# Start of an attention-and-experts kernel: order of the first loads, weight norms from row statistics, first block's roots and the shared splits on VectorE, second block's roots next

## The chip, the cores and the metric

The kernel runs on one core of one Trainium2 chip. The metric is device time in microseconds (us) of one execution; lower is better. The number given for a kernel is the median of its runs.

## The reference

The input x has 4 x 2048 rows of 512. It is layer-normalised to xn, and the output is x + attention(xn) + experts(xn).

- Attention by random features: for a row v, feature r is exp(ab[r] * (v . gs[r]) - 0.5 * |v|^2 * ab[r]^2) times a constant of r, with 512 features. The same function is applied to the 512 rows of `input_weights`, and the output is the product of the rows' features with the features of these weights. So two things are needed of each set of rows: its product with `proj_matrix`, and its squared norms.
- Experts: scores over 64 experts in 8 groups, the best 4 groups, the best 8 experts in them, at most 256 rows per expert; for every expert silu(gate) * up and a down product; plus one shared expert for all rows.

```
dot_products = einsum('...d,rd->...r', xw, ab[:, None] * gs)
correction = (0.5 * sum(xw * xw, axis=-1))[..., None] * (ab * ab)
return 1.0 / sqrt(NUM_RFS) * AB * exp(dot_products - correction)
```

## The kernel before, in words

Tensors are float32. Every large product is made of three passes on TensorE: each operand is split into a rounded high part (`upper`, L96, a cast on ScalarE) and a rest (`rest`, L99, a subtraction, on VectorE unless it is told otherwise), and `products` (L102) multiplies high by high, high by low and low by high.

The rows are worked in 16 blocks of 512 (4 tiles of 128). For each block:

- `normalize` (L252): row statistics on VectorE (`bn_stats`, L257, `bn_aggr`, L261), then the inverse root of the variance in `inverse_root` (L221): two integer operations on VectorE for a first guess (L225, L226) and three Newton steps of four tiny GpSimd operations each (L228 to L231). Two more GpSimd operations make `shift` (L268, L269), three the squared norms (L271 to L273). Then ScalarE writes the four normalised tiles `xw` (L276).
- `look_up` (L309): a generator. Its first step turns the block (`turn`, L291: 16 transposes on TensorE through PSUM, L299, four casts on ScalarE and four subtractions on VectorE give `xT_h` and `xT_l`). Later steps make the router's logits (`ps_l`, L327), copy them (`lt`, L337), turn them back (`ps_lt`, L344) and choose groups and experts with many VectorE operations (L352 to L401), count rows per expert (`ps_b`, `ps_u`, L406, L417) and store the normalised rows and the counts.
- `dense` (L473), for even blocks before the experts: shared gate and up products (`ps_gu`, 48 matmuls), the features (`ps_f`, 48 matmuls, each group of 12 followed by `exponent`, L450, on VectorE and an Exp on ScalarE), and the shared down and attention products (`ps_o`). Odd blocks get this between and after the experts.

`routing` (L790) is called after each step of `dense`; it moves the generators on, starts a block's `look_up` at a step counted by GAP = 5, and calls `normalize` for the block after it. After the 16 blocks, 64 experts follow, then a rest.

The order on each engine comes from the tile framework, which schedules what the program lists and what its dependencies and `behind` (L116: an order without a wait) demand. Every engine works through its list in order. [...]

What is before the first block (L158 to L175 and L572 to L630):

- Loads on the SP queue, in this order: `xis`, `proj_matrix` (`pj`), `input_weights` (`wi`), block 0, router weights, the three shared weights (`sgu` twice, `sd`). Then 1.1 MB of zero rows are written. Block 1 is loaded after the weights' products have been listed (L616).
- `pT` and `wT` are turned from `pj` and `wi`. The weights' squared norms are four ScalarE squares with an accumulator (L583); they are padded, transposed on VectorE, written to `norms` in memory by four small DMAs (`as_row`, L238) and read back over all partitions (`across`, L246: tile `q`).
- The weights' projection: four groups of 12 matmuls `ps_f` in the pool `ps_mm`, each followed by `exponent` into `fw` (L452), which needs `q`.
- The rests of the shared weights are made on GpSimd:

```
    shared_gu = split_gates(sgu, nc.gpsimd, (squared, root))
    ...
    shared_w = shared_gu, split_down(sd, nc.gpsimd)
```

PSUM has three pools: `ps_tr` (2 tiles), `ps_mm` (4) and `ps_sm` (2).

Of the kernel before, what the change touches and what calls it, by code (L numbers as in the profile page):

```python
# [9 lines left out]
FP = mybir.dt.float32  # L10
# [42 lines left out]
def rfs_attention_moe_kernel(  # L53
# [106 lines left out]
    nc.sync.dma_start(ab, xis.rearrange("(c p) -> p c", p=P))  # L160
    pj = load_rows(proj, "pj")
    wi = load_rows(iw, "wi")
# [4 lines left out]
    def load_shared():  # L167
        sgu = [kib4([P, KC, I], "sgu", FP) for _ in range(2)]
        for t, w in zip(sgu, (sgw, suw)):
            nc.sync.dma_start(t, w.rearrange("(c p) i -> p c i", p=P))  # L170
        sd = kib4([P, IC, H], "sd", FP)
        nc.sync.dma_start(sd, sdw.rearrange("(c p) h -> p c h", p=P))
        return sgu, sd

    sgu, sd = load_shared()  # L175
# [45 lines left out]
    def inverse_root(y, v):  # L221

        a = rt.tile([P, NS], FP, tag="a", name="a", bufs=2)
        yi = y.bitcast(I32)
        nc.vector.tensor_scalar(yi, v.bitcast(I32), 1, None, ALU.logical_shift_right)  # L225
        nc.vector.tensor_scalar(yi, yi, -1.0, float(0x5F3759DF), ALU.mult, ALU.add)  # L226
        for _ in range(3):
            nc.gpsimd.tensor_tensor(a, y, v, ALU.mult)  # L228
            nc.gpsimd.tensor_tensor(a, a, y, ALU.mult)
            nc.gpsimd.tensor_scalar(a, a, -0.5, 1.5, ALU.mult, ALU.add)  # L230
            last["root"] = nc.gpsimd.tensor_tensor(y, a, y, ALU.mult)  # L231
# [20 lines left out]
    def normalize(b):  # L252
        xb = xbs[b]
        mv = rt.tile([P, NS, 2], FP, tag="mv", name="mv", bufs=2)
        for s in range(NS):
            st = rt.tile([P, 6], FP, tag="st", name="st", bufs=4)
            stats = nc.vector.bn_stats(st, xb[s])  # L257
            if b == 0:
                behind(stats, last["rest"])
            last["stats"] = stats  # L260
            nc.vector.bn_aggr(mv[:, s, :], st)  # L261
        ve = rt.tile([P, NS], FP, tag="ve", name="ve", bufs=2)
        nc.vector.tensor_scalar(ve, mv[:, :, 1], EPS, None, ALU.add)
        rstd = rt.tile([P, NS], FP, tag="rstd", name="rstd", bufs=2)
        inverse_root(rstd, ve)

        shift = rt.tile([P, NS], FP, tag="shift", name="shift", bufs=2)
        nc.gpsimd.tensor_tensor(shift, mv[:, :, 0], rstd, ALU.mult)  # L268
        nc.gpsimd.tensor_scalar(shift, shift, -1.0, None, ALU.mult)  # L269
# [3 lines left out]
        nc.gpsimd.tensor_scalar(padded[b % 2][:, :NS], q1, -0.5 * H, None, ALU.mult)  # L273
        xw = [rows.tile([P, NH, XW], FP, tag="xw", name="xw") for _ in range(NS // NH)]
# [34 lines left out]
    def look_up(b):  # L309
# [5 lines left out]
            ((ps_tr, "tr"), (ps_sm, "sm")),  # L315
# [134 lines left out]
    def exponent(dst, v, nsq, rc, ps):  # L450
        products(ps, parts(pT, KC, ts(rc, P)), v, True, True)
        return nc.vector.scalar_tensor_tensor(  # L452
            dst, nsq, ab[:, rc : rc + 1], ps, ALU.mult, ALU.add
        )
# [7 lines left out]
    def feature(fT, v, nsq, rc, ps):  # L462
        f = act.tile([P, TB], FP, tag="t", name="f")
        exponent(f, v, nsq, rc, ps)
        nc.scalar.activation(f, f, AF.Exp, scale=ab[:, rc : rc + 1])
        upper(fT[0][rc], f)
        last["dve"] = rest(fT[1][rc], f, fT[0][rc])
# [103 lines left out]

    pT = turn(lambda s: pj[s], "pT", ((ps_mm, "mm"),))  # L572
    wT = turn(lambda s: wi[s], "wT", ((ps_tr, "tr"), (ps_sm, "sm")))
# [4 lines left out]
    normed[0] = normalize(0)  # L578
    first, root = last["stats"], last["root"]
    wq = const.tile([P, NS], FP, name="wq")  # L580
    for s in range(NS):
        sq = act.tile([P, H], FP, tag="t", name="sq")
        squared = nc.scalar.activation(sq, wi[s], AF.Square, accum_out=wq[:, s : s + 1])  # L583
        behind(squared, last["upper"])
    nc.vector.tensor_scalar(padded[2][:, :NS], wq, -0.5, None, ALU.mult)
    as_row(NB, padded[2])
    wn = across(NB)

    def split_gates(gu, on=nc.vector, after=None):
        hi = [kib4([P, KC, I], "gu_h") for _ in range(2)]  # L590
        lo = [kib4([P, KC, I], "gu_l") for _ in range(2)]
        for n in range(2):
            a = upper(hi[n], gu[n])
            b = rest(lo[n], gu[n], hi[n], on)
            if after is not None:
                behind(a, after[0])
                behind(b, after[1])
        return hi, lo

    def split_down(d, on=nc.vector):  # L600
        dh = kib4([P, IC, H], "d_h")
        dl = kib4([P, IC, H], "d_l")
        upper(dh, d)
        rest(dl, d, dh, on)
        return dh, dl

    shared_gu = split_gates(sgu, nc.gpsimd, (squared, root))
    fw = Chunks(RC, "fw", FP)
    for rc in range(RC):
        ps = ps_mm.tile([P, H], FP, tag="mm", name="ps_f")  # L610
        exponent(fw[rc], parts(wT, KC), wn, rc, ps)
# [4 lines left out]
    xbs[1] = load_tokens(1)  # L616
    late = look_up(0)
    next(late)
    normed[1] = normalize(1)
    next(late)  # L620
    next(late)
    shared_w = shared_gu, split_down(sd, nc.gpsimd)
    fW = Chunks(RC, "fW_h"), Chunks(RC, "fW_l")

    def features_w(rc):
        f = fw[rc]
        nc.scalar.activation(f, f, AF.Exp, scale=ab[:, rc : rc + 1])
# [162 lines left out]
    def routing(t):  # L790
# [5 lines left out]
        if k == 0 and b < NB:  # L796
            fronts[b] = look_up(b)
            next(fronts[b])
        if k == GAP - 3 and b + 1 < NB:
            normed[b + 1] = normalize(b + 1)  # L800
# [35 lines left out]
    def ends():  # L836
# [15 lines left out]
        raw, w = load_shared(), []  # L852
# [85 lines left out]
```

## Time and profile before

| | |
|---|---|
| median of 3 runs | 1355.71 us (1353.23 to 1357.19) |
| profiled execution | 1351.38 us, span 1349.6 us |
| TensorE busy | 1322.5 us (98% of the span) |
| VectorE busy | 919.5 us (68%) |
| ScalarE busy | 647.1 us (48%) |
| GpSimd busy | 580.0 us (43%) |
| mean granted clock of TensorE | 0.993 |

The profile is of one execution. In it PE is TensorE's matmul, PEld its weight load, DVE VectorE, ACT ScalarE, POOL GpSimd, SP the queue that issues most DMAs. L12 is line 12 of the kernel. A line of the timeline has the start, the length, the engine, the line, the operation, out<-in with shapes, and in brackets the idle time before it with what ended it. A line of the stages has the stretch, its length, and busy time (count) of PE, the granted clock, the share of time in which the DMA engines were busy, and what they moved; where it lists all engines, they are PE, PEld, DVE, ACT and POOL in that order. A line of the waits has who waited for whom, us in total, how often, and the longest.

### The profile page before, as it was taken

The page shows a single profiled execution, that of the slowest core. Times are in us where ns is not written, and L with a number is a line of the kernel's source. Part 1 is how long each engine was busy: PE and PEld are TensorE (multiplying, and loading weights), DVE is VectorE, ACT ScalarE, POOL GpSimd, SP SyncE. Part 2 cuts the span into 40 slices and gives each one's busy share as a digit, 9 for nine tenths or more (in the row PEclk, how much of TensorE's full clock was granted, in tenths as well). Part 3 has the DMA queues.
Part 4 walks back from the last instruction along what each step waited for, and adds up shares of the span by engine and source line. Part 5 has one row for each costly group of instructions (what it writes and reads, how often), then busy time and mean ns, then how long its engine had stood idle before and what let it go on. Part 6 is the DMA issues. An engine that isn't in the chain of part 4 may idle for free.

```text
span 1349.6 us, 21219 instructions
## 1 busy us (share of the span) xinstructions
PE 1322.5 (98%) x7648; PEld 1153.4 (85%) x7648; DVE 919.5 (68%) x1898; ACT 647.1 (48%) x1025; POOL 580.0 (43%) x683
## 2 busy tenths in 40 slices
PE   7899999999999899999999999999999999999998
PEld 5788888888888799999999999999999999978886
DVE  5887768768765577767677777767776776544455
ACT  5554433443432365556555655655665566531111
POOL 3322022022004566777667676767677655220000
PEclk9899999999999999999999999999999999999999
DMA  7464544564476899999999999999999989756995
GB/s 248 173 231 166 211 184 157 210 222 161 169 268 200 261 243 286 277 270 272 289 268 257 299 287 263 247 283 286 266 263 289 280 235 273 200 143 231 306 316 203
DMA packets 186265, 327.06 MB, mean 242 GB/s; under 512 B 15536, under 2 KB 87216, under 8 KB 186160
## 3 DMA queue, kind: packets, MB, share of 16 engines
q1 hardware_dynamic: 153392, 245.93, 53.0%
q0 software_dynamic: 32768, 79.78, 26.6%
q8 instruction: 60, 0.98, 0.3%
q14 instruction: 45, 0.37, 0.1%
HBM read 220.66 MB, written 104.99 MB: 241 GB/s over the span
## 4 chain that ended last, share of the span: by engine, by line
PE 91%; DMA 3%; DVE 2%; POOL 2%; ACT 1%; issue 1%; SPq 0%; DVEq 0%; POOLq 0%; ACTq 0%
PE ps_gu L107 40%; PE ps_e L107 13%; PE ps_o L107 13%; PE ps_f L107 6%; PE ps_y L107 5%; PE ps_fu L107 5%; PE ps_t L717 4%; PE ps_l L327 2%; PE ps_x L299 2%; DMA at<-upto,line 1%; DMA rw_sb<-in_L_ffn_router_w_dram 1%; POOL at L649 1%; DMA xT_l<-turned 1%; PE ps_lt L344 0%; DVE r L460 0%
## 5 line engine op out<-in xcount | busy, mean ns | idle before, releaser
L107 PE MATMUL ps_gu<-gT,gu_h 128*128 128x256 f32 x2048 | 295.1, 284 | 0.0
L767 POOL DMA_INDIRECT out_dram<-ye,who x128 | 217.4, 1698 | 142.0 <-DMA out_dram<-ye,who 41.1
L107 PEld LDWEIGHTS ps_gu<-gT,gu_h 128*128 128x128 f32 x2048 | 269.3, 192 | 7.0 <-ACT gu_h L97 2.5
L702 POOL DMA_INDIRECT xg<-xnw,who x128 | 143.4, 1121 | 96.1 <-issue 72.1
L649 POOL DMA_INDIRECT at<-upto,line x128 | 148.0, 1156 | 82.5 <-DVE xb L506 43.8
L107 PE MATMUL ps_gu<-gT,gu_l 128*128 128x256 f32 x1024 | 167.1, 285 | 0.0
L100 DVE TENSOR_TENSOR gu_l<-gu,gu_h 128x1024 fp32r<-128x1024 f32 x128 | 155.4, 1216 | 3.8 <-ACT gu_h L97 3.8
L107 PE MATMUL ps_e<-d_h,ehT 128*128 128x512 f32 x512 | 148.8, 392 | 0.0
L107 PEld LDWEIGHTS ps_gu<-gT,gu_l 128*128 128x128 f32 x1024 | 140.9, 192 | 2.8 <-DVE gu_l L100 2.7
L97 ACT CAST gu_h<-gu 128x1024 fp32r<-128x1024 f32 x128 | 131.5, 1056 | 0.0
L97 ACT CAST ehT<-sg 128x512 fp32r<-128x512 f32 x64 | 39.8, 622 | 179.2 <-DVE sg L460 179.2
L228 POOL TENSOR_TENSOR a<-rstd,ve 128x4 f32<-128x4 f32 x48 | 10.9, 227 | 265.4 <-DVE rstd L226 262.8
L107 PEld LDWEIGHTS ps_e<-d_h,ehT 128*128 128x128 f32 x512 | 94.9, 188 | 19.0
L766 ACT ACTIVATE ye<-ps_e,we 128x512 f32<-128x512 f32 x128 | 87.9, 693 | 33.9 <-PE ps_e L107 33.9
L460 DVE SCALAR_TENSOR_TENSOR sg<-sg,ps_gu 128x512 f32<-128x512 f32 x64 | 44.0, 688 | 81.5 <-PE ps_gu L107 81.2
L100 DVE TENSOR_TENSOR d_l<-d,d_h 128x1024 fp32r<-128x1024 f32 x64 | 78.2, 1222 | 11.3 <-ACT d_h L97 11.2
L458 ACT ACTIVATE sg<-ps_gu 128x512 f32<-128x512 f32 x64 | 38.2, 597 | 96.2 <-PE ps_gu L107 95.6
L100 DVE TENSOR_TENSOR gT<-ps_t,gT 128x512 fp32r<-128x512 f32 x128 | 83.3, 682 | 0.4 <-ACT gT L97 0.4
L107 PE MATMUL ps_e<-d_l,ehT 128*128 128x512 f32 x256 | 79.1, 390 | 1.0 <-DVE d_l L100 1.0
L107 PE MATMUL ps_o<-fW_h,fT 128*128 128x512 f32 x288 | 79.7, 391 | 0.3 <-ACT fT L97 0.2
L107 PE MATMUL ps_o<-d_h,hT 128*128 128x512 f32 x256 | 79.8, 399 | 0.0
L717 PE MATMUL ps_t<-ident,xg 128*128 128x128 f32 x512 | 76.1, 275 | 3.5 <-DVE gT L100 3.5
(172 smaller groups left out, 2534.2 us busy)
## 6 DMA issues: line engine op xcount, KB each, us to landing
gu<-in_L_ffn_gate_w_dram SPq DMA_DIRECT2D x64, 512.0 KB
gu<-in_L_ffn_up_w_dram SPq DMA_DIRECT2D x64, 512.0 KB
d<-in_L_ffn_down_w_dram SPq DMA_DIRECT2D x64, 512.0 KB
xnw<-xw SPq DMA_DIRECT2D x32, 577.0 KB
xb<-in_L_attn_x_dram SPq DMA_DIRECT2D x32, 512.0 KB
out_dram<-xb SPq DMA_DIRECT2D x32, 512.0 KB
xT_h<-turned SPq DMA_DIRECT2D x30, 512.0 KB
xT_l<-turned SPq DMA_DIRECT2D x30, 512.0 KB
```

Of the source, the lines that this page charges most:

```text
L97: return nc.scalar.copy(dst, src)
L100: return on.tensor_tensor(dst, src, hi.bitcast(FP), ALU.subtract)
L107: last["pe"] = nc.tensor.matmul(ps, w[c][a], v[c][b], start=(start and part == 0 and c == 0), stop=(stop and part == 2 and c == n - 1),)
L299: last["turn"] = nc.tensor.transpose(ps[:, ts(s, P)], src(s)[:, ts(kc, P)], ident)
L327: logits = nc.tensor.matmul(pl, rwp[:, kc].rearrange("p t e -> p (t e)"), v[kc], start=(n == 0 and kc == 0), stop=(n == 1 and kc == KC - 1),)
L458: nc.scalar.activation(dst, g, AF.Tanh, scale=0.5)
L460: nc.vector.scalar_tensor_tensor(dst, dst, 0.5, u, ALU.mult, ALU.mult)
L649: nc.gpsimd.indirect_dma_start(out=at[:, e % TE, h, :], out_offset=None, in_=upto, in_offset=bass.IndirectOffsetOnAxis(ap=line[:, e, h : h ...
L702: nc.gpsimd.indirect_dma_start(out=xgs[e][:, h, :], out_offset=None, in_=xnw, in_offset=bass.IndirectOffsetOnAxis(ap=who[:, e, h : h + 1], ...
L717: turned_s = nc.tensor.transpose(ps[:, c, ts(h, P)], xg[:, h, ts(c2 * 2 + c, P)], ident)
L766: nc.scalar.activation(ye[:, h, :], po, AF.Copy, scale=wes[e][:, h : h + 1])
L767: now = nc.gpsimd.indirect_dma_start(out=out, out_offset=bass.IndirectOffsetOnAxis(ap=who[:, e, h : h + 1], axis=0), in_=ye[:, h, :], in_o ...
```

## The change

- Loads: `wi` before `pj`; block 1 after the router weights and before the shared weights.
- The weights' squared norms come from `bn_stats` and `bn_aggr` on VectorE (mean squared plus variance, times 512, on GpSimd) in place of the four ScalarE squares. `wT` is turned before `pT`.
- `normalize` is cut into `statistics`, `roots` and the rest. Block 0's Newton steps and its `shift` are on VectorE; all other blocks' stay on GpSimd. Block 1's statistics and roots are listed right after block 0's.
- All three rests of the shared weights are on VectorE: gate's behind block 1's first guess, up's and down's behind block 0's `xT_l`. The casts of up and down go behind block 0's `xT_h`.
- The weights' projection uses `ps_sm` and `ps_tr`, and its `exponent` goes behind block 0's `xT_l`; block 0 is turned through `ps_mm`. 
- Block 1's `look_up` starts one step later.

On the engines: in the changed program GpSimd has 14 operations fewer and VectorE 24 more; on ScalarE the four squares are gone. From VectorE's 180th operation or so on (block 2), the lists of all engines are those of before.

```
+    wi = load_rows(iw, "wi")
     pj = load_rows(proj, "pj")
-    wi = load_rows(iw, "wi")
...
+    xbs[1] = load_tokens(1)
+    sgu = load_shared_gates()
+    sd = load_shared_down()
...
-    def inverse_root(y, v):
+    def inverse_root(y, v, on):
...
-            nc.gpsimd.tensor_tensor(a, y, v, ALU.mult)
-            nc.gpsimd.tensor_tensor(a, a, y, ALU.mult)
-            nc.gpsimd.tensor_scalar(a, a, -0.5, 1.5, ALU.mult, ALU.add)
-            last["root"] = nc.gpsimd.tensor_tensor(y, a, y, ALU.mult)
+            on.tensor_tensor(a, y, v, ALU.mult)
+            on.tensor_tensor(a, a, y, ALU.mult)
+            on.tensor_scalar(a, a, -0.5, 1.5, ALU.mult, ALU.add)
+            on.tensor_tensor(y, a, y, ALU.mult)
...
-            ((ps_tr, "tr"), (ps_sm, "sm")),
+            ((ps_tr, "tr"), (ps_sm, "sm")) if b else ((ps_mm, "mm"),),
...
+    wmv = statistics(wi)
+    wT = turn(lambda s: wi[s], "wT", ((ps_tr, "tr"), (ps_sm, "sm")))
+    wq = const.tile([P, NS], FP, name="wq")
+    nc.gpsimd.tensor_tensor(wq, wmv[:, :, 0], wmv[:, :, 0], ALU.mult)
+    nc.gpsimd.tensor_tensor(wq, wq, wmv[:, :, 1], ALU.add)
+    nc.gpsimd.tensor_scalar(padded[2][:, :NS], wq, -0.5 * H, None, ALU.mult)
...
-    normed[0] = normalize(0)
-    first, root = last["stats"], last["root"]
-    wq = const.tile([P, NS], FP, name="wq")
-    for s in range(NS):
-        sq = act.tile([P, H], FP, tag="t", name="sq")
-        squared = nc.scalar.activation(sq, wi[s], AF.Square, accum_out=wq[:, s : s + 1])
-        behind(squared, last["upper"])
...
+    normed[0] = normalize(0, *roots(0, statistics(xbs[0], NS * [last["rest"]]), nc.vector))
+    first = last["shift"]
+    roots1 = roots(1, statistics(xbs[1], NS * [first]))
+    seed1 = last["seed"]
+
+    def split(t, name, after=(None, None)):
+
+        hi, lo = kib4(list(t.shape), name + "_h"), kib4(list(t.shape), name + "_l")
+        for a, b in zip((upper(hi, t), rest(lo, t, hi)), after):
+            if b is not None:
+                behind(a, b)
+        return hi, lo
...
-    shared_gu = split_gates(sgu, nc.gpsimd, (squared, root))
+    sgate = split(sgu[0], "gu", (None, seed1))
+    ps_w = []
+    for rc in range(RC):
+        pool, tag = ((ps_sm, "sm"), (ps_tr, "tr"))[rc // 2]
+        ps_w.append(pool.tile([P, H], FP, tag=tag, name="ps_f"))
+        projected(parts(wT, KC), rc, ps_w[rc])
+    late = look_up(0)
+    next(late)
+    upper0 = last["upper"]
+    sup = split(sgu[1], "gu", (upper0, last["rest"]))
+    shared_w = list(zip(sgate, sup)), split(sd, "d", (upper0, last["rest"]))
     fw = Chunks(RC, "fw", FP)
     for rc in range(RC):
-        ps = ps_mm.tile([P, H], FP, tag="mm", name="ps_f")
-        exponent(fw[rc], parts(wT, KC), wn, rc, ps)
+        behind(exponent(fw[rc], wn, rc, ps_w[rc]), last["rest"])
+    normed[1] = normalize(1, *roots1)
...
-    xbs[1] = load_tokens(1)
-    late = look_up(0)
-    next(late)
-    normed[1] = normalize(1)
...
-    shared_w = shared_gu, split_down(sd, nc.gpsimd)
...
-        if k == 0 and b < NB:
+        if k == (b == 1) and b < NB:
...
-            normed[b + 1] = normalize(b + 1)
+            normed[b + 1] = normalize(b + 1, *roots(b + 1, statistics(xbs[b + 1])))
```

## Prediction

> **What bounds it now.** I read the first part of the page, then TensorE's waits, then the first 100 us by stages, then the timeline around TensorE's gaps.
>
> ```profile
> span 1349.6 us, 21219 instructions
> PE 1322.5 (98%) x7648; PEld 1153.4 (85%) x7648; DVE 919.5 (68%) x1898; ACT 647.1 (48%) x1025; POOL 580.0 (43%) x683
> ```
>
> TensorE is busy for all but 27 us. Its waits:
>
> ```profile
> PE ps_x L299 <- ACT xw L276: 6.9, 5, 4.5
> PE ps_x L299 <- DMA pj<-_L_attn_proj_matrix_dram: 5.9, 2, 5.3
> ```
>
> 5.9 us are the first load; 6.9 us are waits for the normalised tiles of blocks 0 and 1. By stages (TensorE alone, then all engines):
>
> ```profile
> 23.20:26.60 3.40, 1.01 (x4) 0.93 0.84 305
> 26.60:29.70 3.10, 3.08 (x14) 0.52 0.79 297
> ...
> 39.70:44.20 4.50, 0.03 (x2) 0.89 0.34 124
> 44.20:49.20 5.00, 5.00 (x20) 0.50 0.00 0
> ```
>
> ```profile
> 60.00:70.00 10.00, 10.00 (x51) 8.01 (x50) 9.43 (x23) 7.95 (x16) 4.58 (x17) 1.00 0.77 276
> 70.00:80.00 10.00, 9.97 (x50) 7.89 (x49) 10.00 (x43) 3.87 (x9) 0.00 (x0) 1.00 0.38 130
> 80.00:90.00 10.00, 10.00 (x47) 8.22 (x46) 9.57 (x41) 4.64 (x9) 6.44 (x29) 1.00 0.57 207
> ```
>
> Each wait is followed by a stretch at half the clock (0.52, 0.50). And from 60 to 90 us VectorE is as full as TensorE: there it has little room for a lead. What ends the waits:
>
> ```profile
> 17.47 0.20 POOL L228 TENSOR_TENSOR a<-rstd,ve 128x4 f32<-128x4 f32 x1 [2.72 <-DVE rstd L226]
> 17.75 0.20 POOL L229 TENSOR_TENSOR a<-a,rstd 128x4 f32<-128x4 f32 x1
> ...
> 20.70 2.39 POOL L100 TENSOR_TENSOR gu_l<-sgu,gu_h 128x1024 fp32r<-128x1024 f32 x1
> ...
> 23.64 2.93 ACT L276 ACTIVATE xw<-xb,shift,rstd 128x512 f32<-128x512 f32 x4 [5.35 <-POOL shift L269]
> ...
> 25.41 2.73 DVE L452 SCALAR_TENSOR_TENSOR fw<-q,ab,ps_f 128x512 f32<-128x512 f32 x4 [8.02 <-DMA q<-norms]
> ...
> 36.62 2.36 DVE L226 TENSOR_SCALAR rstd<-rstd 128x4 int32<-128x4 int32 x1
> ...
> 43.32 2.93 ACT L276 ACTIVATE xw<-xb,shift,rstd 128x512 f32<-128x512 f32 x4 [6.14 <-POOL shift L269]
> ```
>
> Block 0's roots run on GpSimd at one operation per 0.28 us (17.47 to 17.75) and have a 2.4 us shared split among them. Block 1's come late: statistics on VectorE at 32.03, the first guess (L226) held for 2.36 us beside GpSimd's split of `sd`, then roots to 43.3.
>
> What the two gaps cost: without waits, 16 transposes take 1.7 us (the row at 93.20). Gap A: products of weights end at 23.2, block 0's first product starts at 29.54, so 29.54 - 23.2 - 1.75 = 4.6 us. Gap B: from 39.56 to 50.15 TensorE does 16 transposes and 7 matmuls, 1.75 + 7 x 0.227 = 3.35 us, so 10.6 - 3.35 = 7.2 us. Together 11.8 us, the most that the change can give.
>
> **The change, part by part.**
>
> Loads. `wi` takes `pj`'s place (5.3 and 6.5 us), `pj` that of `wi` (10.2). TensorE's first 32 transposes keep their times. The four `bn_stats` with aggregates of `wi` (4 x 0.66 + 4 x 0.16 = 3.3 us) fill 5.3 to 8.3, where VectorE is idle (its first split is at 7.91); it is back in step at `pT_l`, 11.3 to 13.8, as `wT_l` before. Block 0's statistics stay at 13.8 to 16.7. The ScalarE squares (2.5 us) are hidden now and are worth nothing. Later loads: before, 5.97 MB have moved by 19.5 us at about 350 GB/s; block 1's 1.05 MB goes ahead of the shared weights and puts these 3 us later: first gate at about 17, `sd` at 19.5, zero rows until 22.5. Their casts are needed from 25 us on, so this is covered.
>
> Block 0's roots on VectorE. 12 + 2 operations. No row has this form on VectorE; the nearest, L225 to L226 (17.02 to 17.22), are dependent and tiny too: 0.20 us. The bounds are 0.17 (the duration alone) and 0.28 (GpSimd's). 14 x 0.20 = 2.8 us: 17.25 to 20.05. `xw` then takes 20.1 to 23.0 and is there when the weights' products end at 23.2. Gap A's wait goes, and with it the cold stretch; transposes end at 24.95.
>
> What is late next: ScalarE's casts `xT_h` (0.56 each, the last at 25.95) and `gu_h` of up (27.0). VectorE has block 1's statistics first (20.05 to 22.8, guess to 23.3), gate's rest (1.22, from the row of the same form at L100 for experts, in place of GpSimd's 2.39) to 24.55, `xT_l` 4 x 0.62 to 27.0. The first 24 gate and up matmuls (5.45 us) end at 30.9: 0.5 us lost.
>
> Block 1's roots stay on GpSimd, from 23.3. At 0.28 each 14 take 3.9 us. Here a rule speaks against the change: the Trainium skill's GPSIMD Engine Reference (Key points) says that GpSimd shares its SBUF interfaces with VectorE and contends with its instructions that read two SBUF inputs. VectorE now does such rests just here. The trace agrees: at 62.58 L228 took 0.52 us and not 0.20 beside `fW_l`. If all 14 ran at 0.6 per step, roots would end at 31.7 and not 27.2. But `xT_l` reads PSUM for one input; only gate's rest (1.2 us) is of that kind, so I take 28.0. `xw` of block 1 ends at 31.9 with the cast of `sd` among it; by the rule alone at 35.6, still before TensorE asks for it at 39. The rest of `sd` would wait for its cast, though, and VectorE with it: 3.7 us of VectorE's lead, kept for the range.
>
> VectorE goes on: up's rest to 28.2, waits for `d_h`, rest of `sd` 29.75 to 31.0, four `fw` (0.68 each) to 33.7. These need `q`. Before, `norms` to `q` took 16.95 to 25.4, 8.5 us. Now it queues behind the loads (22.5) with the 1 MB store of block 1 between: about 29 to 32. I take no loss; upper bound 3 us, behind which the whole queue of VectorE waits.
>
> ScalarE then does three Exp of `fw` ahead of the copy `lt`: it ends at 34.3, TensorE wants it at 33.6: 0.75 us lost. Gate and up end at 39.35; block 1's transposes need no wait: 41.1. Gap B is gone, and features start at 41.1 instead of 52.2: 11.1 us ahead.
>
> VectorE isn't that far ahead. It has taken 3.3 (statistics of `wi`), 2.8 (roots), 3 x 1.22 (rests) on, and lost L226's 2.2 us of standstill: 7.6 us more work. Counting its list on from 33.7 by these durations, `xT_l` of block 1 ends at 48.3 (53.3 before); router logits wait 1.3 us. Features end at 55.9 (66.07). Block 0's last feature is at 61.0 and its cast at 62.3; TensorE wants it at 60.45: 1.85. Block 2's `xw` (roots on GpSimd from 56.7) is 0.75 late. Its `xT_l` ends at 72.7 (76.8 before); the logits wait 1.1 us more. They end at 72.95 against 80.71, and ps_b and ps_u (0.5) come later: TensorE is 7.3 us ahead. After that, in block 2, VectorE has 0.5 to 1.4 us of idle time before most of its steps (90 to 100 us: 6.1 busy), so it binds no more, and the lists are those of before. The start of block 1's `look_up` one step later is in this count.
>
> Does the half clock come back? The Trainium skill's TensorE: Matmul & The Clock Gate (Part 1) puts the fall to half at an idle window of about 3.4 us. My waits are up to 1.85 us, so by it nothing is lost. But the row from 23.20 cooled it with 1.01 us busy in 3.40; were that to happen once more, the 3.1 us at 0.52 would cost 1.5 us. I charge nothing and keep 1.5 for the range.
>
> Sum: 11.1 at the features, less the waits of 1.3, 1.85, 0.75 and 1.1, plus 1.2 of small losses of before in this stretch (slow mixed transposes): 7.3 us. The profiled execution took 1351.38 us, 1.8 more than its span; so 1344.1 there. It lies 4.3 under the median of the runs; the same gain on the median: 1355.7 - 7.3 = 1348.4.
>
> **Rivals.**
> - VectorE keeps up (0.22): its order puts routing behind what TensorE needs, or steps are shorter than my 0.62 and 0.66. Then all but 1.3 us of the 11.8 stay: 1345.2. For it: the gaps are real and wholly at the start. Against: 9.4, 10.0 and 9.6 of 10 us busy.
> - VectorE holds more (0.18): `q` is 3 us late, or roots run at 0.6, or the clock falls once; 7.3 - 3 to 5: about 1352.7.
> - Slower (0.05): `q`. VectorE works in order, and four `fw` stand ahead of all of block 0's gating. Each us that `q` comes after 31 takes one off both leads. At 38.3 nothing is left; for 0.3% slower it must land at 42.4. For it: the wait of 8.02 us before L452. Against: the bytes ahead of it are gone by 25.5. This gives 1356 to 1360.
> - That the wait for `xw` isn't removed: `sgu`'s cast stands ahead of `xw` on ScalarE; if the load came after 20 us instead of 17, each us is lost. It is part of the third case.
>
> **Numbers.** Likeliest (0.55): 1348.4, own range 1346.3 to 1350.5. A measurement of this kernel tells 0.3% (4 us) from no change. Faster by more: 0.53 of the first, 0.22, and 0.04 of "holds more": 0.79. Within: 0.16. Slower: 0.05. The range 1343.5 to 1352.7 leaves out the slower case, half of "holds more" and a little below.
>
> **What would show it.** `xw` of block 0 starting near 20 us; TensorE without a wait at 23.2 and at 40; clock 1.00 from 15 to 60; features of block 0 starting near 41; `q` landing before 31; TensorE waiting, in all, some 6 us between 25 and 75, mostly for VectorE's splits and ScalarE's copies; block 2's first product near 80.5 instead of 87.75. I am wrong if `q` is what `fw` waits for by more than 2 us, if VectorE is idle over 2 us between 35 and 70, or if the lead at 88 us isn't kept to the end.

## The result, and the profile after

| | before | after |
|---|---|---|
| median | 1353.95 us (1353.23 to 1357.19, 6 runs) | 1343.75 us (1342.57 to 1344.87, 6 runs) |
| profiled execution | 1351.38 us, span 1349.6 us | 1344.87 us, span 1343.1 us |
| VectorE busy | 919.5 us | 924.4 us |
| TensorE busy | 1322.5 us | 1318.5 us |

The ratio is 0.992, 95% interval 0.9907 to 0.9932: 10.2 us between the medians, where 7.3 us were forecast. The median that the forecast started from, of three runs, was also a high one: three more runs took it from 1355.71 to 1353.95 us. So of the 4.65 us between the forecast of 1348.4 and the 1343.75 measured, 1.76 are the base and 2.9 the gain. The two profiled executions differ by only 6.5 us; the last point of the list in the explanation says why.

The page of the changed kernel, first lines, then TensorE's waits (us in total, times, longest; smaller ones left out):

```profile
span 1343.1 us, 21213 instructions
PE 1318.5 (98%) x7648; PEld 1152.6 (86%) x7648; DVE 924.4 (69%) x1922; ACT 645.5 (48%) x1017; POOL 583.0 (43%) x669
```

```profile
PE ps_x L313 <- DMA wi<-_attn_input_weights_dram: 6.2, 2, 5.5
PE ps_t L736 <- DVE gT L100: 5.7, 1, 5.7
PE ps_l L341 <- DVE fw L468: 2.2, 1, 2.2
```

The 6.9 us of waits for `xw` are gone from the list. A wait of 2.2 us is new: the router's logits `ps_l`, which multiply `xT_h` and `rwp`, wait for `fw` on VectorE. The first wait, for the first load, is as before.

The stages of the changed kernel (stretch, length, busy time and count of PE, PEld, DVE, ACT and POOL, then the granted clock, DMA share and GB/s):

```profile
23.00:44.00 21.00, 18.42 (x91) 15.04 (x90) 16.66 (x31) 14.30 (x26) 5.21 (x17) 0.92 0.37 110
44.20:58.00 13.80, 13.80 (x68) 11.49 (x66) 13.80 (x47) 7.75 (x16) 0.77 (x2) 1.00 0.76 267
58.00:79.40 21.40, 21.40 (x108) 17.52 (x107) 21.23 (x78) 9.50 (x19) 8.56 (x32) 1.00 0.64 222
```

The first stretch in the kernel before:

```profile
23.00:44.00 21.00, 14.31 (x62) 10.99 (x61) 17.95 (x48) 10.77 (x19) 9.47 (x25) 0.90 0.48 168
```

In the first stretch TensorE was busy for 14.31 us in the kernel before, now for 18.42. From 44 us to block 2 (79.4) it never stops, though VectorE has hardly a pause either (13.80 of 13.80, 21.23 of 21.40). That is the opposite of the forecast, which had TensorE waiting for VectorE just there.

The timeline around the start (start, length, engine, line, operation, and in brackets the idle time before):

```profile
17.27 0.16 DVE L235 TENSOR_TENSOR a<-rstd,ve 128x4 f32<-128x4 f32 x1
17.46 0.16 DVE L236 TENSOR_TENSOR a<-a,rstd 128x4 f32<-128x4 f32 x1
...
20.06 2.94 ACT L290 ACTIVATE xw<-xb,shift,rstd 128x512 f32<-128x512 f32 x4 [1.95 <-DVE shift L279]
22.88 1.91 PE L313 MATMUL ps_x<-ident,xw 128*128 128x128 f32 x16
23.28 1.23 DVE L100 TENSOR_TENSOR gu_l<-sgu,gu_h 128x1024 fp32r<-128x1024 f32 x1
23.45 1.11 POOL L235 TENSOR_TENSOR a<-rstd,ve 128x4 f32<-128x4 f32 x1 [2.94 <-DVE rstd L231]
24.64 0.20 POOL L236 TENSOR_TENSOR a<-a,rstd 128x4 f32<-128x4 f32 x1
...
26.82 1.22 DVE L100 TENSOR_TENSOR gu_l<-sgu,gu_h 128x1024 fp32r<-128x1024 f32 x1
26.88 1.21 POOL L236 TENSOR_TENSOR a<-a,rstd 128x4 f32<-128x4 f32 x1
...
29.29 0.81 ACT L290 ACTIVATE xw<-xb,shift,rstd 128x512 f32<-128x512 f32 x1 [2.78 <-POOL shift L279]
30.01 1.03 ACT L97 CAST d_h<-sd 128x1024 fp32r<-128x1024 f32 x1
31.08 1.23 DVE L100 TENSOR_TENSOR d_l<-sd,d_h 128x1024 fp32r<-128x1024 f32 x1 [2.92 <-ACT d_h L97]
32.22 2.72 DVE L468 SCALAR_TENSOR_TENSOR fw<-q,ab,ps_f 128x512 f32<-128x512 f32 x4
33.11 1.29 PE L341 MATMUL ps_l<-xT_h,rwp 128*128 128x512 f32 x4 [2.21 <-DVE fw L468]
```

Three things are to be seen. Block 0's roots run on VectorE at one per 0.20 us, and `xw` starts at 20.06. Block 1's roots on GpSimd, 0.20 us each, have two steps that lasted 1.11 and 1.21 us, each beside a rest `gu_l` on VectorE of that length. And from the last of them a chain hangs that ends on TensorE: GpSimd's `shift` (29.26) lets ScalarE start block 1's `xw` (29.29), the cast `d_h` comes next in ScalarE's list (30.01), VectorE stood idle for 2.92 us for it, the rest of `sd` (31.08) and then `fw` (32.22) follow, and only `fw` frees a tile of `ps_sm` that the weights' projection holds and `ps_l` needs (33.11). It was the change that put this projection into `ps_sm` and `ps_tr`.

### The profile page after: what moved, and what is told of

Read it like the earlier page. It is cut to its first block, busy times and chain, and to the rows that moved or that the text cites. A ratio compares the mean times of both kernels' runs of the same rounds, so it can differ in the third digit from the quotient of the medians.

```text
span 1343.1 us, 21213 instructions
## 1 busy us (share of the span) xinstructions
PE 1318.5 (98%) x7648; PEld 1152.6 (86%) x7648; DVE 924.4 (69%) x1922; ACT 645.5 (48%) x1017; POOL 583.0 (43%) x669
## 4 chain that ended last, share of the span: by engine, by line
PE 91%; DMA 3%; DVE 3%; POOL 1%; issue 1%; ACT 1%; SPq 0%; DVEq 0%; POOLq 0%; ACTq 0%
PE ps_gu L107 40%; PE ps_e L107 13%; PE ps_o L107 13%; PE ps_f L107 6%; PE ps_y L107 5%; PE ps_fu L107 5%; PE ps_t L736 4%; PE ps_l L341 2%; PE ps_x L313 2%; DMA at<-upto,line 1%; DMA xT_l<-turned 1%; PE ps_lt L358 0%; POOL at L668 0%; DMA xg<-xnw,who 0%; DMA wi<-_attn_input_weights_dram 0%
## 5 line engine op out<-in xcount | busy, mean ns | idle before, releaser
L786 POOL DMA_INDIRECT out_dram<-ye,who x128 | 223.7, 1748 | 142.4 <-DMA out_dram<-ye,who 42.1
L668 POOL DMA_INDIRECT at<-upto,line x128 | 151.8, 1186 | 82.2 <-DVE first_of L662 43.5
```

Of the source, the lines that this page charges most:

```text
L668: nc.gpsimd.indirect_dma_start(out=at[:, e % TE, h, :], out_offset=None, in_=upto, in_offset=bass.IndirectOffsetOnAxis(ap=line[:, e, h : h ...
L786: now = nc.gpsimd.indirect_dma_start(out=out, out_offset=bass.IndirectOffsetOnAxis(ap=who[:, e, h : h + 1], axis=0), in_=ye[:, h, :], in_o ...
```

## The experiments

Two theories are weighed here. **Chain**: what sets TensorE from 25 to 44 us is block 1's chain (statistics, roots on GpSimd held by VectorE's rests, `xw`, and what is queued behind it); after that VectorE has slack. **VectorE**: as in the prediction, VectorE's list sets TensorE from 48 us on. The main yardsticks are the start of block 0's gate products, of the logits `ps_l`, of block 0's features, and of block 2's first product, from the timelines:

| kernel | ratio to before (95%) | gate | `ps_l` | features | block 2 |
|---|---|---|---|---|---|
| before_again | 0.9997 (0.9988 to 1.0006) | 30.17 | 32.14 | 52.49 | 88.05 |
| after_again | 0.9916 (0.9903 to 0.9930) | 25.20 | 33.15 | 44.23 | 79.41 |
| roots_on_gpsimd | 0.9908 (0.9896 to 0.9921) | 27.66 | 33.35 | 42.79 | 78.23 |
| block1_late | 0.9951 (0.9938 to 0.9964) | 26.70 | 31.92 | 40.15 | 80.51 |
| fw_first | 0.9939 (0.9920 to 0.9958) | 25.46 | 29.43 | 44.55 | 80.06 |
| roots_gpsimd_fw_first | 0.9925 (0.9908 to 0.9942) | 27.64 | 31.72 | 42.74 | 77.99 |
| splits_on_gpsimd | 0.9923 (0.9909 to 0.9937) | 28.02 | 32.33 | 43.86 | 79.48 |
| squares_on_scalare | 0.9938 (0.9922 to 0.9954) | 26.70 | 34.66 | 44.21 | 79.61 |
| after_third_chip | 0.9928 (0.9914 to 0.9943) | 25.21 | 33.15 | 44.24 | 79.41 |
| roots_gpsimd_fw_first_again | 0.9916 (0.9902 to 0.9930) | 27.37 | 31.43 | 42.48 | 77.85 |
| gate_rest_after_shift | 0.9907 (0.9890 to 0.9923) | 25.89 | 29.97 | 40.99 | 76.22 |
| vector_load | 0.9934 (0.9919 to 0.9948) | 25.38 | 33.33 | 44.43 | 79.60 |

The first four ran on one chip (before there 1353.74 us), the next four on a second (before there 1364.00 us), the last four on a third (1353.63 us). On the second chip the stage of the first experts took longer: from the first `ps_fu` (near 409 us) to the first `ps_e` 56.4 to 62.1 us, in all other traces 49.9 to 52.9. Ratios of different chips are not compared; the starts in the timelines agree between chips within 0.3 us. One distance helps to read the table: from gate to features TensorE takes 15.1 us in the kernels without a wait for `ps_l` or `lt` and without a fall of the clock there (roots_on_gpsimd, roots_gpsimd_fw_first, gate_rest_after_shift) and 19.0 us in the changed kernel. All edits below are against the changed kernel and compute all that it computes.

**before_again and after_again**: the two kernels, unchanged.

> The kernel before once more, for a second trace of it. Theory (the gain is made in the first 80 us; what differs later differs from execution to execution): ratio 1.000 within 0.002; block 2's first product at 87.75 within 0.3 us, as in the first trace; but TensorE's wait for the first experts' rows (3.54 us in the first trace of before, 5.73 in that of after) comes out anywhere from 1 to 7 us. Rival (that wait depends on the kernel): it is 3.5 within 0.5 here again.

> The changed kernel once more. Theory: ratio 0.992 within 0.0015; block 2's first product at 79.3 within 0.3 us, the wait for ps_l on fw 2.2 us again, and the wait for the first experts' rows not 5.7 but again anywhere from 1 to 7. Rival: that wait is 5.7 within 0.5 again, so the change gives 2 us back there.

Measured: 1353.22 and 1343.76 us. The lead of 8.6 us at block 2 is 9.3 us at the first expert (444.4 and 435.1 us), and the spans are 1352.7 and 1342.9 us: 9.8 apart.

**roots_on_gpsimd**: block 0's roots and `shift` back on GpSimd, all else as changed.

```
-    normed[0] = normalize(0, *roots(0, statistics(xbs[0], NS * [last["rest"]]), nc.vector))
-    first = last["shift"]
+    normed[0] = normalize(0, *roots(0, statistics(xbs[0], NS * [last["rest"]]), nc.gpsimd))
+    first = last["seed"]
```

> The changed kernel with only block 0's Newton steps and shift back on GpSimd; the splits stay on VectorE, so no split stands among them. Theory: 14 steps at 0.28 instead of 0.20 us, so block 0's xw starts 1.1 us later, at about 21.2, and TensorE waits about 1.1 us at 23: 1 us slower than the changed kernel, 1344.8. Rival (the engine of the roots is what gap A was about): 3 to 5 us slower, 1347 to 1349.

Measured: 1342.11 us against 1343.76. The expected 1 us slower failed. The intervals overlap, so time alone says only that it is not slower; the trace says that it is 1.2 us ahead at block 2. Its timeline:

```profile
17.94 1.28 DVE L264 BATCH_NORM_STATS2 st<-xb 128x6 f32<-128x512 f32 x2
...
21.28 1.23 DVE L100 TENSOR_TENSOR gu_l<-sgu,gu_h 128x1024 fp32r<-128x1024 f32 x1
21.50 1.06 POOL L278 TENSOR_TENSOR shift<-mv,rstd 128x4 f32<-128x4 f32 x1
...
32.12 2.71 DVE L468 SCALAR_TENSOR_TENSOR fw<-q,ab,ps_f 128x512 f32<-128x512 f32 x4
```

Block 1's statistics start at 17.94 instead of 19.93: VectorE goes on to them while GpSimd does block 0's roots, and block 1's roots are done at 27.2 instead of 29.26. But this brings `fw` hardly forward (32.12 instead of 32.27): ScalarE now casts up first and starts block 1's `xw` at 29.16 instead of 29.34. What differs is TensorE. Block 0 comes 2.5 us later (gate 27.66 instead of 25.20), TensorE is at `ps_l` at 33.35, when its tile has just come free, and the clock stays at 1.00. The changed kernel comes early, waits 2.2 us, starts `ps_l` at 33.15, and then loses the clock: features come 11.1 us after `ps_l` there, 9.4 us here. So the roots on VectorE won 2.5 us for block 0, which were waited away, and after the wait the clock fell. They are not a source of the gain. The third case of a step held for VectorE's rest (1.06 us beside 1.23) is here.

**block1_late**: block 1's statistics and roots only after the shared splits, as the kernel before had them late.

```
-    roots1 = roots(1, statistics(xbs[1], NS * [first]))
...
-    normed[1] = normalize(1, *roots1)
+    normed[1] = normalize(1, *roots(1, statistics(xbs[1], NS * [last["rest"]])))
```

> The changed kernel with block 1's statistics and roots listed again after the weights' exponents; all else is kept. Theory: gap B comes back in part: statistics on VectorE from 31 to 34, roots on GpSimd to 39 or 40, xw to 43 while TensorE is there at 40, so a wait of 2 to 3 us and a stretch at half the clock: 3 to 6 us slower, 1347 to 1350. Rival (gap B was closed by taking the splits off GpSimd alone): within 1 us of the changed kernel.

Measured: 1346.95 us, 3.2 over the changed kernel. TensorE's wait is back at block 1's transposes; `ps_l` (31.92) has none:

```profile
44.07 0.66 PE L313 MATMUL ps_x<-ident,xw 128*128 128x128 f32 x4 [3.08 <-ACT xw L290]
```

(Features stand ahead of that wait in this kernel's list, so their 40.15 says nothing.) No half clock followed this wait: granted 1.00 from 44 to 50 us.

The edit did more than move block 1. `seed1` now means block 0's first guess, so VectorE made gate's rest ahead of block 0's roots; `shift` ended at 21.94 instead of 20.03, and gate starts 1.5 us later. It also took block 1's `xw` away from in front of `d_h`, and with it the wait for `ps_l`. And trace and time differ: block 2 and the first expert come only 1.1 and 1.0 us later than in after_again, while the medians are 3.2 us apart, with intervals that don't overlap (the trace is of the fastest of five executions, 1344.29 us, that of after_again of the slowest of its six). So early roots for block 1, with the wait that they bring, are worth 1 us in the first stages; where the other 2 us come from is not shown.

**fw_first**: the four `fw` ahead of the rest of `sd` in VectorE's list.

```
-    shared_w = list(zip(sgate, sup)), split(sd, "d", (upper0, last["rest"]))
...
-        behind(exponent(fw[rc], wn, rc, ps_w[rc]), last["rest"])
+        last["fw"] = exponent(fw[rc], wn, rc, ps_w[rc])
+        behind(last["fw"], last["rest"])
+    shared_w = list(zip(sgate, sup)), split(sd, "d", (upper0, last["fw"]))
```

> The changed kernel with one thing moved: the four exponents fw stand ahead of the rest of sd on VectorE (and sd's cast moves behind block 1's xw on ScalarE). Theory (the new wait of 2.2 us for ps_l, and the stretch at 0.62 of the clock after it, come from the PSUM tiles that fw holds while VectorE waits for sd's cast): both go, features start near 40.5 instead of 44.2. If VectorE then binds, as the prediction had it, TensorE gets new waits of some 2 us between 40 and 70 and is at block 2 near 77.5: 1342. If it doesn't, block 2 starts near 75.7: 1340. Rival (the wait is for the load of q): fw starts no earlier than 31 and nothing changes.

Measured: `ps_l` starts at 29.43 without a wait, and nothing is won. Features start at 44.55. ScalarE's timeline and TensorE's:

```profile
29.60 2.94 ACT L290 ACTIVATE xw<-xb,shift,rstd 128x512 f32<-128x512 f32 x4 [2.65 <-POOL shift L279]
...
33.05 1.03 ACT L97 CAST d_h<-sd 128x1024 fp32r<-128x1024 f32 x1
33.98 0.58 ACT L351 COPY lt<-ps_l 128x512 f32<-128x512 f32 x1
```

```profile
34.61 0.90 PE L358 MATMUL ps_lt<-ident,lt 128*128 128x128 f32 x4 [2.25 <-ACT lt L351]
```

The wait moved one step on: the logits are there, but their copy `lt` stands in ScalarE's list behind block 1's `xw`, an Exp and `d_h`, all of which stand behind the same GpSimd `shift` (29.56). It is 2.25 us now instead of 2.21, and the half clock follows it too. The expected 40.5 us failed. By the traces both waits hang from the late `shift` of block 1, through ScalarE's list.

**roots_gpsimd_fw_first**: the two edits above together.

> Both of the above: block 0's roots on GpSimd and fw ahead of the rest of sd. Theory: roots on VectorE only pay once the wait behind them is gone; so this is 1 us slower than fw ahead alone (about 1.1 us of wait at 23 comes back, with no cold stretch): block 2 near 77.5 to 78. Rival (VectorE's load is what binds): it is 1 to 2 us faster than fw ahead alone, since 2.8 us leave VectorE.

Measured: 1353.40 us where fw_first took 1356.44 on the same chip; block 2 at 77.99, 2.1 us before it. TensorE waits only 1.0 us, for block 0's `xw`, and the clock is 1.00 from 15 to 54 us. Again the chain's end did not move much (behind the cast of up ScalarE starts block 1's `xw` at 29.14 instead of 29.60, and `lt` at 33.75 instead of 33.98): TensorE comes to it 2.2 us later, so it has nothing to wait for and keeps the clock. The expected 77.5 to 78 came, but not the expected order of the two kernels.

**splits_on_gpsimd**: the three rests of the shared weights on GpSimd, as before the change.

```
-    sgate = split(sgu[0], "gu", (None, seed1))
+    sgate = split(sgu[0], "gu", (None, None), nc.gpsimd)
...
+    sup = split(sgu[1], "gu", (upper0, None), nc.gpsimd)
+    shared_w = list(zip(sgate, sup)), split(sd, "d", (upper0, None), nc.gpsimd)
...
-        behind(exponent(fw[rc], wn, rc, ps_w[rc]), last["rest"])
+        behind(exponent(fw[rc], wn, rc, ps_w[rc]), rest0)
```

(`rest0` is block 0's last `xT_l`.)

> The changed kernel with the three rests of the shared weights back on GpSimd: gate's at 18, before block 1's roots, up's and sd's behind them. Theory: VectorE loses 3.7 us of work and fw no longer stands behind sd's cast, so ps_l doesn't wait; but up's rest comes at about 31.5 and TensorE wants it at 29.8, and sd's is done by 34 while block 0's lists need it at 58: net 1 to 2 us faster than the changed kernel, 1342. Rival (the move of the splits to VectorE is where the gain came from): 3 us slower or more, with block 1's roots held up on GpSimd.

Measured: 1353.06 us; block 2 at 79.48, within 0.15 us of the changed kernel. GpSimd's steps are not held here: block 1's 14 run 0.28 us apart and are done at 30.57. But the hold has only changed sides. GpSimd's timeline and VectorE's:

```profile
18.66 2.40 POOL L100 TENSOR_TENSOR gu_l<-sgu,gu_h 128x1024 fp32r<-128x1024 f32 x1 [3.26 <-ACT gu_h L97]
```

```profile
18.83 2.25 DVE L237 TENSOR_SCALAR a<-a 128x4 f32<-128x4 f32 x1
21.12 0.16 DVE L238 TENSOR_TENSOR rstd<-a,rstd 128x4 f32<-128x4 f32 x1
```

Gate's rest on GpSimd (to 21.06) holds a step of block 0's roots on VectorE for 2.25 us instead of 0.17. So block 0's `xw` starts at 23.30 instead of 20.06, gate at 28.02, and block 1's roots at 26.69. With that loss block 2 is where it was, since `ps_l` has no wait and the clock doesn't fall. The rival (3 us slower) is out; what the place of the rests is worth without the hold, this run doesn't tell.

**squares_on_scalare**: the weights' squared norms by four ScalarE squares again, and `pT` turned ahead of the norms.

```
-    wmv = statistics(wi)
+    for s in range(NS):
+        sq = act.tile([P, H], FP, tag="t", name="sq")
+        squared = nc.scalar.activation(sq, wi[s], AF.Square, accum_out=wq[:, s : s + 1])
+        behind(squared, last["upper"])
...
```

> The changed kernel with the weights' norms from ScalarE's squares again. Theory: VectorE's 3.3 us lay in its idle time before 8.3 and the squares lie in ScalarE's idle time before 17, so block 0 stays where it is; q lands later (norms written from 17 on instead of 12), near 29 to 31, just before fw at 32.2: within 1 us of the changed kernel. Rival (q is at the edge): q lands after 32.2, fw and ps_l move by as much, 1 to 3 us slower.

Measured: block 2 at 79.61, 0.2 us from the changed kernel. That this edit costs nothing would be the wrong reading. Block 0's `shift` ends 1.5 us later (21.57 instead of 20.03; VectorE stands 0.54 us for a ScalarE square among block 0's statistics), and `ps_l` starts 1.5 us later (34.66 instead of 33.15), after a wait of 2.2 us as well. The stages behind that wait, first of this kernel, then of the changed one:

```profile
34.60:38.50 3.90, 3.84 (x19) 3.11 (x20) 3.62 (x7) 3.65 (x8) 0.00 (x0) 1.00 0.84 278
```

```profile
33.10:37.00 3.90, 3.89 (x11) 3.10 (x12) 3.03 (x6) 2.79 (x6) 0.00 (x0) 0.62 0.85 280
```

After the same wait 19 matmuls run in 3.9 us here and 11 there. The half clock did not fall here, and that gave back the 1.5 us. So the statistics of the weights, with the order of turning, did help; the clock hid it.

**after_third_chip, roots_gpsimd_fw_first_again**: the yardstick and the best so far side by side.

> The changed kernel once more, as the yardstick for the three others beside it. Block 2's first product near 79.4 us, as in both traces so far (79.33 and 79.41); 0.992 of the kernel before.

> Block 0's roots on GpSimd and fw ahead of the rest of sd, now on the same chip as the changed kernel. My theory (block 1's roots set when TensorE gets to the features, and block 0's roots on VectorE push them 2 us back): block 2's first product at 78.0, 1.4 us before the changed kernel's, and about 1.4 us less in time. The rival, that the end is set by later waits whatever the lead at block 2: the same time within 0.5 us.

Measured: 1344.26 and 1342.55 us, block 2 at 79.41 and 77.85. The lead of 1.56 us at block 2 is 1.7 us at the end; the intervals of the times overlap, the traces agree with it (1.70 at the first expert). The numbers came as expected; that it is block 1's roots that do it is not shown, since `lt` (33.47) is no more than half a us earlier than in fw_first.

**gate_rest_after_shift**: the kernel roots_gpsimd_fw_first, and gate's rest on VectorE waits for block 0's `shift` on GpSimd.

```
+    shift0 = last["shift"]
...
+        if wait is not None:
+            tc.add_manual_dep(a.ins, wait.ins.name, AFTER, reason="not beside the roots")
...
+    sgate = split(sgu[0], "gu", (None, seed1), shift0)
```

> As the kernel beside it with block 0's roots on GpSimd, but gate's rest waits until block 0's shift is done, so that no step of these roots runs beside it. If the rest's two SBUF inputs are what held one of these steps for 1.06 us, block 0's xw starts 0.9 us earlier, TensorE's first gate product is at 26.8 and block 2's first product near 77.1. If the step would be held by something else, gate at 27.6 and block 2 at 78.0, as without it. If VectorE binds between 45 and 75 us, gate is earlier but block 2 stays at 78.0.

Measured: 1341.48 us, the lowest median of the three beside it (its interval overlaps those of the others); gate at 25.89, block 2 at 76.22, 1.6 us before the kernel without the wait, where some 0.9 was expected. Of the 1.48 us by which `xw` starts earlier (21.17 and 22.65), 0.58 were there already when the roots began (17.20 and 17.78: the statistics started earlier by as much, with the same list), and some 0.9 are the hold. Its timelines, GpSimd and VectorE:

```profile
20.90 0.24 POOL L279 TENSOR_SCALAR shift<-shift 128x4 f32<-128x4 f32 x1
21.10 0.20 POOL L282 TENSOR_TENSOR q<-q,rstd 128x4 f32<-128x4 f32 x1
21.39 1.09 POOL L283 TENSOR_SCALAR padded<-q 128x4 f32<-128x4 f32 x1
22.45 0.19 POOL L235 TENSOR_TENSOR a<-rstd,ve 128x4 f32<-128x4 f32 x1
```

```profile
21.17 1.22 DVE L100 TENSOR_TENSOR gu_l<-sgu,gu_h 128x1024 fp32r<-128x1024 f32 x1 [0.71 <-POOL shift L279]
```

The rest was moved by some 0.2 us, from 21.00 to 21.17, and the hold moved with it: in the kernel without the wait `shift` took 1.13 us, here its two steps take 0.20 and 0.24, and `padded`, which `xw` doesn't wait for, takes 1.09. So it is this rest that holds GpSimd, to the rest's end, and whichever step meets it pays. Features start at 40.99, where the prediction had them (41.1), and still TensorE waits for nothing from 40 to 80 us.

**vector_load**: four unused `bn_stats` in VectorE's list, one behind each of block 0's feature rests.

```
+            spare = rt.tile([P, 6], FP, tag="spare", name="spare", bufs=4)
+            behind(nc.vector.bn_stats(spare, fT[0][rc].bitcast(FP)), last["dve"])
```

> The changed kernel with four more bn_stats (0.66 us each, 2.6 us in all, their results unused) in VectorE's list beside block 0's features. Nothing is left out of the computation. My theory now (VectorE is full there but has slack, TensorE comes too late to wait for it): block 2's first product within 0.7 us of 79.4. The prediction's reasoning (VectorE's list is what TensorE follows from 48 us on): block 2 later by most of the 2.6 us, near 82, with TensorE waits for VectorE's tiles between 45 and 80 us.

Measured: block 2 at 79.60, 0.2 us later; in 40 to 80 us TensorE's matmuls wait for nothing, and a weight load once for VectorE, 0.2 us. The extra steps ran at 55 to 68 us, 0.68 us each, and `xT_l` of block 2 ended 1.4 us later (72.4), not 2.7: the framework's schedule also put routing steps of VectorE behind it, and block 2's logits later in TensorE's list (71.10 instead of 69.74, with `ps_o` products ahead of them). So it isn't VectorE's list alone that was changed, and the run does not measure the slack cleanly. It shows that TensorE has other products to put there. The 0.2 us grew to 0.9 us by block 2's features (93.45 and 92.58) and to 1.1 us by the first expert, with a wait of 0.38 us for block 3's `xw`: the slack is not without end.

## Why the prediction was right about the cause and wrong about the size

The forecast's mechanism, two gaps closed for some 11 us, held. The step that failed is the one behind it: that VectorE, being behind, makes TensorE wait 5.0 us between the features of block 0 and block 2. It made it wait for none. A second term failed the other way: a wait of 2.2 us in front of `ps_l`, with the loss of the clock behind it, was put at nothing. In the forecast's own sum, 11.1 - 5.0 + 1.2 = 7.3 us of lead at block 2 became 8.0 - 0 + 0.4 = 8.4. The lead of TensorE over the kernel before, forecast and measured in the first pair of traces:

| at | forecast | measured | from |
|---|---|---|---|
| gate products of block 0 | 4.6 | 4.4 | 29.54 - 25.16 |
| features of block 0 | 11.1 | 8.0 | 52.20 - 44.19 |
| block 2 | 7.3 | 8.4 | 87.75 - 79.33 |
| first expert | 7.3 | 9.0 | 444.1 - 435.1 |

- **Loads, statistics, roots on VectorE** (to 20.05): right. `shift` ended at 20.03, and the wait for `xw` at 23.2 is gone.
- **"I take no loss" for `q`**: right, and its term was generous. In fw_first the first `fw` started at 28.25 without waiting for it, so it had landed before the forecast's 29 to 32.
- **Block 1's roots at 28.0**: 29.26. The term allowed 0.8 us of contention, in gate's rest alone, as steps of 0.6 us. In fact one step is held to the end of that rest, and up's rest, which the forecast's own list had at 27.0 to 28.2, beside the last steps, held a second: 1.11 and 1.21 us instead of 0.20. This is the rule of the Trainium skill weighed in the prediction (GPSIMD Engine Reference, Key points); it was the right rule, and 1.1 of the 1.26 us are a price taken too small. The row that the forecast read for the price shows why. GpSimd and VectorE in the kernel before:

```profile
62.58 0.52 POOL L228 TENSOR_TENSOR a<-rstd,ve 128x4 f32<-128x4 f32 x1
63.17 0.52 POOL L229 TENSOR_TENSOR a<-a,rstd 128x4 f32<-128x4 f32 x1
```

```profile
62.30 1.33 DVE L100 TENSOR_TENSOR fT<-f,fT 128x512 fp32r<-128x512 f32 x2 [0.57 <-ACT fT L97]
63.56 1.28 DVE L100 TENSOR_TENSOR fW_l<-fw,fW_h 128x512 fp32r<-128x512 f32 x2
```

At 62.58 the step meets `fT` (0.68 us each), not `fW_l`, and it ends just after the first `fT`: 63.10. The next ends after the second, at 63.69. So 0.52 was no slower pace but what was left of VectorE's instruction, and beside a rest of 1.22 us it is up to 1.2. In gate_rest_after_shift the held step is one that doesn't count; splits_on_gpsimd turns the hold round.
- **"Block 1's transposes need no wait: 41.1"**: they had none, but `ps_l` ahead of them had. The forecast followed data, and not the PSUM tile: the weights' projection was moved to `ps_sm`, so `ps_l` waits for `fw`, and `fw` stood behind `d_l`, `d_h` and block 1's `xw`. The prediction had priced `lt` for 0.75 us there. TensorE lost 2.21 us, and then the clock. That the tile is what `ps_l` waited for is shown by fw_first, where `fw` comes earlier and `ps_l` doesn't wait.
- **The half clock**, "I charge nothing and keep 1.5 for the range": failed. In the changed kernel:

```profile
34.00:35.00 1.00, 1.00 (x4) 0.76 (x3) 1.00 (x3) 1.00 (x2) 0.00 (x0) 0.50 0.99 336
...
36.00:37.00 1.00, 1.00 (x4) 0.81 (x3) 0.13 (x1) 0.86 (x2) 0.00 (x0) 0.50 0.49 190
37.00:38.00 1.00, 1.00 (x7) 0.79 (x7) 0.74 (x2) 0.84 (x2) 0.00 (x0) 0.79 0.07 27
```

That is 3.4 us at half speed, so 1.7 us lost; 2.21 + 1.7 are the 3.9 us by which this kernel takes longer from gate to features than those without a wait (19.0 and 15.1). Put in place of 0.75 they are the 3.1 us by which features came late. Every stretch at half clock that the traces show from 10 to 60 and from 440 to 475 us lasted 3.4 us, or two or three times as long, however long the wait before it was.
- **The rule behind the half clock**: the one that the forecast rested on (the Trainium skill's TensorE: Matmul & The Clock Gate, Part 1: a fall to half after an idle window of about 3.4 us), taken as a threshold on one wait, is against these runs: after 2.21 and 2.25 us the clock fell, after another 2.2 us and after 3.08 us it did not. And in the kernel before it fell at the first gap in one trace (0.52, the row in the prediction) and stayed at 1.00 in the other (before_again, 24 to 30 us), where the transposes came 0.6 us later; the gate products then waited 1.28 us for `xT_h` and came 0.6 us later too. So at that gap the half clock cost little, if anything. Where a wait lies seems to count: in the four traces with it at 31 to 33.3 us (three of the changed kernel, and vector_load) the clock fell and features come 11.1 us after `ps_l` each time, and in squares_on_scalare, with it 1.5 us later and no fall, 9.55. The page also says that the window runs free of the kernel, which would make it a matter of where a wait falls; no run here shows the window itself.
- **VectorE behind: 1.3 + 1.85 + 0.75 + 1.1 = 5.0 us of waits**: failed by the most. From 40 to 80 us TensorE waited for nothing in the changed kernel, nor in any other traced kernel with block 1's roots early, but for 0.2 us in splits_on_gpsimd. (The term "plus 1.2 of small losses" was worth 0.4: 35.55 us from features to block 2 before, 35.14 after.) Two causes can be told. TensorE came to it 3.1 us later, by the wait above. And VectorE's list was counted too long: from the last `xT_l` of block 1 to that of block 2 the forecast has 72.7 - 48.3 = 24.4 us, the trace 71.0 - 49.85 = 21.15. The durations in the timeline overlap:

```profile
52.86 0.66 DVE L264 BATCH_NORM_STATS2 st<-xb 128x6 f32<-128x512 f32 x1
53.44 0.16 DVE L267 BATCH_NORM_AGGREGATE mv<-st 128x2 f32<-128x6 f32 x1
53.52 0.71 DVE L468 SCALAR_TENSOR_TENSOR f<-q,ab,ps_f 128x512 f32<-128x512 f32 x1
54.15 0.68 DVE L100 TENSOR_TENSOR fT<-f,fT 128x512 fp32r<-128x512 f32 x1
54.76 0.17 DVE L267 BATCH_NORM_AGGREGATE mv<-st 128x2 f32<-128x6 f32 x1
```

A `bn_stats` of 0.66 us lets the next start after 0.58, an aggregate of 0.16 after 0.08, a rest of 0.68 after 0.61. The durations of the 71 operations in that stretch add up to 27.0 us, in 21.15 us of time. The forecast had taken the distance for some forms (0.62 for `xT_l`) and the duration for others (0.66); that its 3.25 us too many came all from this is an inference that no run shows. gate_rest_after_shift bears on the whole: features at the forecast's time and no wait, so the first cause alone is not it (VectorE was then 3.5 us earlier with `fw` as well, and without block 0's roots). Its way from features to block 2 takes 35.2 us, that of the changed kernel 35.1, that of the kernel before 35.55.

- **"The lead kept to the end"**: it grew by 0.6 us between 88 and 435 us, 0.1 us for each pair of blocks (48.26 us in place of 48.36 in the second pair of traces). What makes the pairs shorter, with the same matmuls and the same single 0.2 us wait, stays open. The 2.9 us of gain beyond the forecast are 1.1 us at block 2, these 0.6, and 1.2 between the traces' lead (9.0) and that of the medians (10.2); the last two stay open.
- **The profiled executions**: at 450 us TensorE waits for the first expert's rows, through `gT`, for 3.5 us (before), 5.6 (before_again), 5.7 (after), 4.3 (after_again) and 5.2 (after_third_chip), each followed by stretches at half clock. The wait differs between executions of one kernel by more than between kernels; the trace of before that was used had the short one, and the shortest stretch at half clock behind it (3.4 us, where the changed kernel's had 6.8). So the lead of 9.0 us at the first expert is 6.1 us at the first `ps_e` (468.2 and 462.1) in this pair. In the kernel before and the changed one (VectorE's step that waits for the rows):

```profile
457.11 1.23 DVE L661 TENSOR_TENSOR at<-at,slot 128x1024 f32<-128x1024 f32 x1 [3.60 <-DMA at<-upto,line]
```

```profile
450.29 1.23 DVE L680 TENSOR_TENSOR at<-at,slot 128x1024 f32<-128x1024 f32 x1 [5.78 <-DMA at<-upto,line]
```

The rivals: "VectorE keeps up" (1345.2) was the one that came nearest, a gain of 10.5 us where 10.2 were measured, and in part for its reason (steps are shorter than counted). But it counts 1.3 us lost where the wait for `ps_l` and the half clock took 3.9, and part of the gain came later, from a source that stays open: its number is luck in part. Slower by `q`: no sign of it.

Which part of the change gives the 10 us? No part could be told by itself. Early roots for block 1 give 1 us by the trace and 3.2 by the medians, with two other things moved (block1_late). The roots of block 0 on VectorE give nothing (roots_on_gpsimd, 1.2 us the other way). For the rests on VectorE nothing is shown (splits_on_gpsimd, with a hold in their place). The statistics of the weights give up to 1.5 (squares_on_scalare). What is left, between 5 and 8 us if these add up, is for the order of loads and of turning and for the way in which the parts work together; that was not tried by itself.

## What to carry to other kernels

When a projection moves to other PSUM tiles, list who needs those tiles next and follow the release back through every queue to its first cause; a data dependency that is met says nothing of it. Count an engine's list by the distance from start to start, not by durations, before it is called the bound. And when one chain is made faster, ask what the next wait leaves of it: here 2.5 us were won for one block and spent waiting for a tile whose chain had not moved, and the clock fell after the wait.

## What the runs showed of the hardware

- A 128x4 step on GpSimd, 0.20 us alone, lasted 1.06 to 1.21 us where it met a VectorE subtraction of two SBUF tiles (1.22 us), in each case to about that one's end (24.56 and 24.51 for the first in the changed kernel): twice in the changed kernel, fw_first, squares_on_scalare and vector_load, once in the two kernels with block 0's roots on GpSimd and in gate_rest_after_shift. Beside `xT_l`, with one input in PSUM, the steps kept 0.20 us.
- It goes the other way too: a 128x4 step on VectorE, 0.17 us alone, lasted 2.25 us beside a subtraction of 2.40 us on GpSimd (splits_on_gpsimd), to that one's end (21.08 and 21.06).
- After waits of about 2.2 us TensorE's clock fell to half in three kernels (the changed one, vector_load, fw_first; from 0.3 to 1.3 us after the wait) and did not in a fourth; after a wait of 3.08 us it did not in a fifth. A stretch at half clock lasted 3.4, 6.8 or, in three traces, 10.2 us.
- On one of three chips the stage of the first experts took 56.4 to 62.1 us in the four kernels traced (49.9 to 52.9 us in the traces of the other two), and the kernel before took 10 us more (1364.00 us).
